# A graph and expert kernel on one core: 96-column products in its sort, table products in two halves, statistics on ScalarE, and byte source rows

## The chip, the cores and the metric

The kernel runs on one core of a Trainium2 chip. A core has five engines with a queue of instructions each, and an engine takes its queue in order: TensorE (PE for matmuls, PEld for its weight loads), VectorE (DVE), ScalarE (ACT), GpSimd (POOL) and SyncE (SP, which only issues DMAs). Semaphores tie the queues together. The metric is the device time of one execution in microseconds (us); lower is better.

## What is computed

A node table `x` (6250 x 256) and 206,250 directed edges (100,000 pairs in both directions and one loop per node) go through two graph attention layers and a mixture of eight experts:

```python
def _gat_layer(x, src, dst, W, b, a, g, beta, N, concat):
    h = x @ W.T + b
    score = (h @ a[:d])[src] + (h @ a[d:])[dst]
    e = jnp.exp(-jax.nn.leaky_relu(score, ALPHA))
    h_prime = jax.ops.segment_sum(e[:, None] * h[dst], src, num_segments=N)
    ...                      # a layer norm of each row, times g, plus beta
x = x + elu(gat(elu(concat(8 heads of gat(layernorm(x))))))
x = x + moe(layernorm(x))    # 8 experts, the best 2 of a softmax for each row
```

The edges are given sorted by `dst`; the sums go by `src`. So the kernel first sorts the edges by blocks of 128 sources.

## The kernel before

It has three stages in a row.

**The sort** (first 427 us) handles all edges in 23 segments (`SEGS`). For each segment DVE finds the edges of each of the 49 blocks (`rows_of_blocks`, L227, `here`), PE counts those in the rows before (`counts_before`, L234) and ACT copies the counts (L237, `up`). DVE weighs `here` with them (`places_before`, L244, `mine`), PE adds them up (`places`, L251), and DVE makes of the sum each edge's place in its run: `both_sides` reduces (L257), adds (L260), writes a one-hot `slot` of 84 places for each of 72 edge columns (L262), two products `what` (L266), and the addresses (L268, L271). Both tiles have their four columns of a group (`KC`) innermost, so a matmul reads them with a step of four f16 elements. `append` multiplies `what` by `slot` in 72 matmuls of 84 columns (L278), ACT copies the runs out of PSUM (L281), and POOL scatters them to `srt` in device memory by four indirect DMAs (L283), each of which waits for the one before to land.

In the same time the sort also makes the first layer's table: a `tick` moves each of the 49 blocks of `x` by one stage. ACT normalizes a block (`normed_x`, L344), PE transposes it (L349), ACT copies (L354), PE multiplies by the weights (`products`, L362: 512 columns of features to `ph` and 16 columns of scores to `pk`, f32, each as two passes for each of two halves of the depth, and a bias product, L363), and ACT copies the two results to `row` (L369, L370) and the scores to `s1` (L371); SP writes `row` to `tab1` (L372). Once for a chunk of seven blocks, `spread` takes mean and variance on DVE (L329, L330), adds epsilon (L332) and takes the root on ACT (L333); two ticks later `scales` makes reciprocal and shift (L337, L339).

The order is written out by hand. In iteration t the stages are emitted as places_before(t+2), rows_of_blocks(t+4), append(t), counts_before(t+3), places(t+2), both_sides(t+1), and after the second, the fourth and the sixth a tick, when one is due by this formula:

```python
if n % 2:
    due = len(ticks) * (3 * (t + 1) + n // 2) // (3 * SEGS)
```

`ticks` runs from -3 to 52; 56 ticks fall on 23 iterations, two or three on each. After the iterations 0, 5 and 10 stands a piece of `lefts` (L221, L222), some 9 us of small DVE operations.

**The two layers** (from 436 us to 2567 us and from 2613 us on) go through the sorted edges in tiles of 128, 34 tiles to a block, in groups of up to five (`GT`). `read_back` (L521) reads three blocks' worth of `srt`, splits source and destination numbers and writes the sources to `srow` (L546, L551). For a group, `sources` broadcasts its row of `srow` to all partitions (`rb`, L643, by SP), `gather` fetches each edge's table row by an indirect DMA on POOL for each tile (L649), `one_hot` compares `rb` with the partition number on DVE (`ot`, L656), PE picks the sources' scores with it (L662), DVE and ACT make the weights (L668, L670, L584, L585), DVE makes messages and a one-hot of destinations in the sum (L684, L687; in the second layer L693), and PE adds them up by source (L705). Stages of later groups are emitted ahead: the gathers six or eight groups, `one_hot` five, `sources` eleven. When a block is complete its layer norm and the next projection follow (L808 to L848 in the first layer); in the second layer the experts run in between (L1019, L1021, L1027).

Of the kernel before, what the change touches and what calls it, by code (L numbers as in the profile page):

```python
# [24 lines left out]
BF16 = mybir.dt.bfloat16  # L25
F16 = mybir.dt.float16
I32 = mybir.dt.int32
AF = mybir.ActivationFunctionType
OP = mybir.AluOpType
AX = mybir.AxisListType  # L30

P = 128
# [4 lines left out]
PITCH = 36  # L37
CHUNK = 18
RUN = 84
KC = 4  # L40


# [6 lines left out]
def kernel(ctx: ExitStack, tc: tile.TileContext, x, src, dst, w_heads, b_heads, a_heads,  # L49
# [20 lines left out]
    REST = E - FULL * EC  # L70
    LO = 2 * W
    PG = 7
    assert P - 16 < FULL < EP and LO < REST and W * PG <= 512
    CAP = TILES * P
    PIT = PITCH * P
    SLOTS = NB * PIT
# [10 lines left out]
    dram = ctx.enter_context(tc.tile_pool(name="dram", bufs=1, space=bass.MemoryType.DRAM))  # L87

    srt = dram.tile([2 * SLOTS + E + RUN, 1], F16, name="srt")
    srow = dram.tile([NB * PIT], BF16, name="srow")  # L90
    tab1 = dram.tile([NB * P + 1, R1], F32, name="tab1")
    ssrc1 = dram.tile([NB * P, H], F32, name="ssrc1")
    ssrc2 = dram.tile([NB * P, 1], F32, name="ssrc2")
# [18 lines left out]
    nc.gpsimd.iota(iota_n, pattern=[[1, P]], base=0, channel_multiplier=0, allow_small_or_imprecise_dtypes=True)  # L112
    iota_p = const.tile([P, 1], F32, name="iota_p")
    nc.gpsimd.iota(iota_p, pattern=[[0, 1]], base=0, channel_multiplier=1, allow_small_or_imprecise_dtypes=True)
    iota_e = const.tile([P, NE], F32, name="iota_e")
    nc.gpsimd.iota(iota_e, pattern=[[1, NE]], base=0, channel_multiplier=0, allow_small_or_imprecise_dtypes=True)
    zero = const.tile([1, R1], F32, name="zero")
# [135 lines left out]
    def both_sides(g):  # L253

        place = sw.tile([EP, W], F16, name="place")
        sums = sw.tile([EP, W], F32, name="sums")
        nc.vector.tensor_reduce(sums.rearrange("p (j k) -> p j k", k=KC),  # L257
                                seg[g]["pos"][:EP, :W * PG].rearrange("p (j b k) -> p j k b", b=PG, k=KC),
                                axis=AX.X, op=OP.add)
        nc.vector.tensor_add(place, sums, left[:, g * W:(g + 1) * W])  # L260
        slot = seg[g]["slot"] = sw.tile([EP, CHUNK, RUN, KC], F16, name="slot")
        nc.vector.tensor_tensor(slot, over(place.rearrange("p (j k) -> p j k", k=KC), RUN), each(place_no, RUN),  # L262
                                op=OP.is_equal)
        for i in range(2):
            what = whats[g % 2][:, :CHUNK * B2, :].rearrange("p (j b) k -> p j b k", b=B2)
            nc.vector.tensor_mul(what[:, :, i * NB:(i + 1) * NB, :], seg[g]["here"], over(by_column(kept[:, i], g), NB))  # L266
        c0 = g * KC
        nc.vector.tensor_tensor_scan(end[:B2, 1 + c0:1 + c0 + KC], count[:B2, c0:c0 + KC], count[:B2, c0:c0 + KC],  # L268
                                     initial=end[:B2, c0:c0 + 1], op0=OP.add, op1=OP.max)
        to = seg[g]["to"] = sw.tile([P, KC], I32, name="to", bufs=4)  # L270
        nc.vector.tensor_copy(to[:B2], end[:B2, c0:c0 + KC])  # L271

    def append(g):

        run_ps = bank("run", "run_ps")
        for k in range(KC):
            for j in range(CHUNK):
                nc.tensor.matmul(run_ps[:, k * RUN:(k + 1) * RUN], whats[g % 2][:, j * B2:j * B2 + P, k], seg[g]["slot"][:, j, :, k],  # L278
                                 start=(j == 0), stop=(j == CHUNK - 1))
        run = sw.tile([P, KC, RUN], F16, name="run", bufs=3)  # L280
        nc.scalar.copy(run[:B2].rearrange("p k r -> p (k r)"), run_ps[:B2, :KC * RUN])  # L281
        for k in range(KC):
            nc.gpsimd.indirect_dma_start(  # L283
                out=srt, out_offset=bass.IndirectOffsetOnAxis(ap=seg[g]["to"][:B2, k:k + 1], axis=0),
                in_=run[:B2, k, :], in_offset=None)
        seg[g] = None
# [28 lines left out]
    def load_x(c):  # L315
# [6 lines left out]
        nc.sync.dma_start(xc[:, :full, :], x[c0 * P:(c0 + full) * P, :].rearrange("(b p) f -> p b f", p=P))  # L322
        chunks[c] = {"x": xc}

    def spread(c):
        st = sw.tile([P, CB, nc.vector.BN_STATS_DIM], F32, name="st")
        mv = chunks[c]["mv"] = sw.tile([P, CB, 2], F32, name="mv")
        for i in range(CB):
            nc.vector.bn_stats(st[:, i, :], chunks[c]["x"][:, i, :])  # L329
            nc.vector.bn_aggr(mv[:, i, :], st[:, i, :])  # L330
        rstd = chunks[c]["rstd"] = sw.tile([P, CB], F32, name="rstd")
        nc.vector.tensor_scalar_add(rstd, mv[:, :, 1], EPS)  # L332
        nc.scalar.activation(rstd, rstd, AF.Sqrt)  # L333

    def scales(c):
        rstd = chunks[c]["rstd"]
        nc.vector.reciprocal(rstd, rstd)  # L337
        shift = chunks[c]["shift"] = sw.tile([P, CB], F32, name="shift")
        nc.vector.scalar_tensor_tensor(shift, chunks[c]["mv"][:, :, 0], -1.0, rstd, op0=OP.mult, op1=OP.mult)  # L339

    def normed_x(b):
        c, i = chunks[b // CB], b % CB
# [14 lines left out]
    def products(b):  # L357
        ph = bank("ph", "ph")
        pk = bank("pk", "pk")
        for to, cols in ((ph, slice(0, HD)), (pk[:, :2 * H], slice(HD, C1))):  # L360
            for k in range(KF):
                nc.tensor.matmul(to, blocks[b][:, k, :], wt[:, k, cols], start=(k == 0), stop=False)  # L362
            nc.tensor.matmul(to, three, bias3[:, cols], start=False, stop=True)  # L363
        blocks[b] = ph, pk

    def table_rows(b):
        ph, pk = blocks.pop(b)
        row = sw.tile([P, C1], F32, name="row", bufs=2)
        nc.scalar.copy(row[:, HD:], pk[:, :2 * H])  # L369
        nc.scalar.copy(row[:, :HD], ph)  # L370
        nc.scalar.copy(s1[:, b, :], row[:, R1:])  # L371
        nc.sync.dma_start(tab1[b * P:(b + 1) * P, :], row[:, :R1])  # L372

    def tick(n):

        for stage, behind in ((table_rows, 4), (products, 3), (turned_copy, 2), (turned_x, 1), (normed_x, 0)):
            if 0 <= n - behind < NB:
                stage(n - behind)
        if (n + 3) % CB == 0 and n + 3 < NB:
            spread((n + 3) // CB)  # L380
        if (n + 1) % CB == 0 and n + 1 < NB:
            scales((n + 1) // CB)
            if (n + 1) // CB + 1 < NB // CB:
                load_x((n + 1) // CB + 1)
# [29 lines left out]
    with tc.manual_schedule():  # L414
# [106 lines left out]
    def read_back(pool, c):  # L521
# [65 lines left out]
    def edges(es, layer, table, sel, ssrc, k, width, block_done, more=None):  # L587
# [573 lines left out]
```

## Time and profile before

| | |
|---|---|
| median of 14 runs | 4847.91 us (4839.64 to 4856.49) |
| the profiled execution | 4843.64 us, its span 4841.9 us |
| mean granted TensorE clock | 0.902 |
| PE, DVE, ACT, POOL busy | 80%, 67%, 27%, 70% of the span |
| last append of the sort, PE | 396.5 to 402.4 us |
| last scatter of the sort, POOL | starts at 426.3 us |
| first and last gather, layer 1 | start at 435.6 and 2566.5 us |
| first and last gather, layer 2 | start at 2613.0 and 4720.0 us |

A line of a group gives line of the kernel, engine, operation, what it writes and reads, shapes and count; after the bar the busy time in us and the mean of one in ns; after the second bar the idle time of the engine just before, and what ended it. A line of a timeline gives start, length, engine, line and operation. Consecutive operations of an engine overlap somewhat, so that the time from start to start can be shorter than the duration of one.

### The profile page before, as it was taken

The page shows a single profiled execution, that of the slowest core. Times are in us where ns is not written, and L with a number is a line of the kernel's source. Part 1 is how long each engine was busy: PE and PEld are TensorE (multiplying, and loading weights), DVE is VectorE, ACT ScalarE, POOL GpSimd, SP SyncE. Part 2 cuts the span into 40 slices and gives each one's busy share as a digit, 9 for nine tenths or more (in the row PEclk, how much of TensorE's full clock was granted, in tenths as well). Part 3 has the DMA queues.
Part 4 walks back from the last instruction along what each step waited for, and adds up shares of the span by engine and source line. Part 5 has one row for each costly group of instructions (what it writes and reads, how often), then busy time and mean ns, then how long its engine had stood idle before and what let it go on. Part 6 is the DMA issues. An engine that isn't in the chain of part 4 may idle for free. (4 is left out here: it accounts for less than half of the span.)

```text
span 4841.9 us, 52631 instructions
## 1 busy us (share of the span) xinstructions
PE 3886.2 (80%) x16462; PEld 2398.0 (50%) x16462; DVE 3259.3 (67%) x8048; ACT 1307.4 (27%) x2440; POOL 3368.0 (70%) x3450
## 2 busy tenths in 40 slices
PE   5995888888888888888885568778877877887888
PEld 3773343343334333343333456555655655655666
DVE  9995778788878887788774445555555555555553
ACT  1221111111111111111111124344433433433442
POOL 2455777777777777777774777777777777777770
PEclk7997999999999999999997779989988989989998
DMA  2214888888888888888885555555555555555540
GB/s 61 72 62 117 239 238 239 236 234 243 241 232 231 246 239 237 230 242 241 235 236 154 135 134 131 139 139 139 132 138 139 131 139 139 132 138 139 136 121 12
DMA packets 378009, 825.33 MB, mean 170 GB/s; under 512 B 91760, under 2 KB 210780, under 8 KB 377719
## 3 DMA queue, kind: packets, MB, share of 16 engines
q0 software_dynamic: 216464, 665.03, 51.5%
q1 hardware_dynamic: 155868, 151.02, 11.1%
q10 hardware_dynamic: 5386, 5.83, 0.4%
q8 instruction: 131, 2.15, 0.2%
q14 instruction: 160, 1.30, 0.1%
HBM read 792.59 MB, written 28.99 MB: 170 GB/s over the span
## 5 line engine op out<-in xcount | busy, mean ns | idle before, releaser
L649 POOL DMA_INDIRECT gt<-tab,dst_idx x3324 | 3181.4, 957 | 1104.8 <-issue 902.2
L705 PE MATMUL acc<-msg,hot 128*128 128x512 f32 x3324 | 1588.3, 629 | 0.0
L670 DVE TENSOR_TENSOR ssum<-ssum,gt 128x40 f32<-128x40 f32 (+3 forms) x684 | 126.9, 186 | 1323.8 <-DMA gt<-tab,dst_idx 1252.3
L705 PEld LDWEIGHTS acc<-msg,hot 128*128 128x128 f32 x3324 | 637.8, 201 | 684.0 <-issue 683.5
L687 DVE TENSOR_TENSOR msg<-gt,ee 128x2560 f32<-128x2560 f32 (+1 forms) x342 | 935.2, 2735 | 0.1
L705 PE MATMUL acc<-gt,hot 128*128 128x256 f32 x3324 | 920.8, 429 | 0.0
L705 PEld LDWEIGHTS acc<-gt,hot 128*128 128x128 f32 x3324 | 680.9, 214 | 100.3 <-issue 0.5
L585 ACT ACTIVATE ee<-lr 128x40 f32<-128x40 f32 (+3 forms) x684 | 141.7, 207 | 1667.2 <-DVE lr L584 1624.4
L585 ACT ACT_TABLE_LOAD x252 | 323.3, 1283 | 834.1 <-DVE lr L584 779.7
L1027 PE MATMUL py<-w2s,h 128*128 128x256 f32 x1568 | 407.1, 408 | 110.5 <-ACT h L1021 67.2
L662 PEld LDWEIGHTS <-ot 128*128 128x128 bf16 x3324 | 187.3, 100 | 588.9 <-issue 309.9
L693 DVE TENSOR_SCALAR hot<-iota_n,sloc,ee 128x128 f32<-128x128 f32 x1662 | 464.8, 357 | 0.9 <-issue 0.5
L662 PE MATMUL ps<-sel,ot 128*128 128x24 bf16 (+1 forms) x3324 | 187.8, 171 | 309.1 <-DVE ssum L668 297.1
L1019 PE MATMUL ph<-tokt,w1s 128*128 128x512 f32 (+1 forms) x832 | 378.0, 584 | 42.9 <-ACT h L1021 41.0
L1027 PEld LDWEIGHTS py<-w2s,h 128*128 128x128 f32 x1568 | 312.1, 203 | 189.9 <-ACT h L1021 75.2
L283 POOL DMA_INDIRECT srt<-run,to x92 | 170.6, 1854 | 245.6 <-DMA srt<-run,to 149.2
L825 PE MATMUL pt<-ident,hc 128*128 128x128 f32 x196 | 52.2, 418 | 285.2 <-DVE hc L821 285.2
L684 DVE TENSOR_TENSOR hot<-iota_ps,sloc 128x640 f32<-128x640 f32 (+1 forms) x342 | 272.8, 798 | 0.0
L656 DVE TENSOR_SCALAR ot<-rb,iota_p 128x640 bf16<-128x640 bf16 (+1 forms) x684 | 264.2, 387 | 7.3 <-DMA rb<-srow 7.3
L1019 PEld LDWEIGHTS ph<-tokt,w1s 128*128 128x128 f32 x832 | 152.8, 195 | 169.2 <-issue 106.1
L1032 DVE SCALAR_TENSOR_TENSOR xq<-py,comb,xq 128x256 f32<-128x256 f32 x392 | 166.8, 474 | 49.9 <-PE py L1027 49.9
L825 PEld LDWEIGHTS pt<-ident,hc 128*128 128x128 f32 x196 | 33.4, 208 | 325.3 <-DVE hc L821 325.3
(248 smaller groups left out, 3391.7 us busy)
## 6 DMA issues: line engine op xcount, KB each, us to landing
rb<-srow SPq DMA_DIRECT2D x588, 160.0 KB
gt<-tab,dst_idx POOLq DMA_INDIRECT x3324
tab<-row SPq DMA_DIRECT2D x49, 260.0 KB
rb<-srow SPq DMA_DIRECT2D x96, 128.0 KB
tab<-row SPq DMA_DIRECT2D x49, 128.5 KB
xq<-in_x_dram SPq DMA_DIRECT2D x12, 512.0 KB
out_dram<-xq SPq DMA_DIRECT2D x12, 512.0 KB
xc<-in_x_dram SPq DMA_DIRECT2D x6, 896.0 KB
```

The costliest lines, as they stand in the source:

```text
L283: nc.gpsimd.indirect_dma_start(out=srt, out_offset=bass.IndirectOffsetOnAxis(ap=seg[g]["to"][:B2, k:k + 1], axis=0), in_=run[:B2, k, :], i ...
L585: nc.scalar.activation(ee, lr, AF.Exp, scale=-1.0)
L649: nc.gpsimd.indirect_dma_start(out=gt[:, j, :], out_offset=None, in_=table, in_offset=bass.IndirectOffsetOnAxis(ap=dst_idx[c][:, t0 + j:t0 ...
L656: nc.vector.tensor_scalar(ot[:, :cols], now[n]["rb"][:, :cols], iota_p, None, op0=OP.is_equal)
L662: nc.tensor.matmul(ps[:, j * 3 * k:(j + 1) * 3 * k], ot[:, j * P:(j + 1) * P], sel[:, groups[n][0]].rearrange("p t k -> p (t k)"), start=T ...
L684: nc.vector.tensor_tensor(hot, iota_ps[:, None, :P].to_broadcast([P, nt, P]), sl[:, :, None].to_broadcast([P, nt, P]), op=OP.is_equal)
L687: nc.vector.tensor_mul(msg.rearrange("p j (h d) -> p j h d", h=k), gt[:, :, :width].rearrange("p j (h d) -> p j h d", h=k), ee[:, :, :, No ...
L693: nc.vector.tensor_scalar(hot[:, j, :], iota_n, sl[:, j:j + 1], ee[:, j, :], op0=OP.is_equal, op1=OP.mult)
L705: nc.tensor.matmul(accs[b][:, :width], now[n]["hot"][:, j, :], now[n]["msg"][:, j, :width], start=(g == 0 and j == 0), stop=False)
L1019: nc.tensor.matmul(ph[:, :W], w1s[:, e, k, f * P:(f + 1) * P], tokt[:, k, :W], start=(k == 0), stop=(k == KF - 1))
L1027: nc.tensor.matmul(py[:, (i - lo) * F:(i - lo + 1) * F], h1[:, k, i * P:(i + 1) * P], w2s[:, e, k, :], start=(k == 0), stop=(k == KF - 1))
L1032: nc.vector.scalar_tensor_tensor(xq[:, i, :], py[:, (i - lo) * F:(i - lo + 1) * F], comb[:, i, e:e + 1], xq[:, i, :], op0=OP.mult, op1=OP.add)
```

## The change

Four edits are made together.

- `append`'s matmuls read 96 columns of `slot` in place of 84. `slot` becomes a pair of fixed tiles with 12 columns of zeros at the end; the extra 12 columns of a matmul are the first of the next row and are written to PSUM and not copied out.
- `products` splits the 528 columns into two halves of 264 rather than 512 and 16; the copies follow.
- Mean and variance come from ACT: a new function `means` sums each block by an ACTIVATE with an accumulator, `spread` sums the squares of the difference in the same way. DVE scales the mean, and scales the sum of squares and adds epsilon. `means` is emitted in the tick two ahead of `spread` (for the first chunk in the same tick), at the end of the tick.
- `srow`, `lb` and `rb` hold bytes, not bf16; the byte is the source's number plus one, and `one_hot` compares it with a partition number plus one.

```diff
+RUN_N = 96
...
-    srow = dram.tile([NB * PIT], BF16, name="srow")
+    srow = dram.tile([NB * PIT], U8, name="srow")
...
+    nc.gpsimd.iota(iota_p1, pattern=[[0, 1]], base=1, channel_multiplier=1, allow_small_or_imprecise_dtypes=True)
...
+    slots = [sp.tile([EP, CHUNK * RUN + RUN_N - RUN, KC], F16, name=f"slot{i}") for i in range(2)]
...
-        slot = seg[g]["slot"] = sw.tile([EP, CHUNK, RUN, KC], F16, name="slot")
+        slot = seg[g]["slot"] = slots[g % 2]
...
-                nc.tensor.matmul(run_ps[:, k * RUN:(k + 1) * RUN], whats[g % 2][:, j * B2:j * B2 + P, k], seg[g]["slot"][:, j, :, k],
+                nc.tensor.matmul(run_ps[:, k * RUN_N:(k + 1) * RUN_N], whats[g % 2][:, j * B2:j * B2 + P, k],
+                                 seg[g]["slot"][:, j * RUN:j * RUN + RUN_N, k],
                                  start=(j == 0), stop=(j == CHUNK - 1))
...
-        nc.scalar.copy(run[:B2].rearrange("p k r -> p (k r)"), run_ps[:B2, :KC * RUN])
+        nc.scalar.copy(run[:B2], run_ps[:B2, :KC * RUN_N].rearrange("p (k r) -> p k r", r=RUN_N)[:, :, :RUN])
...
+    def means(c):
+        x = chunks[c]["x"]
+        mean = chunks[c]["mean"] = sw.tile([P, CB], F32, name="mean")
+        junk = sp.tile([P, F], BF16, name="junk")
+        for i in range(CB):
+            nc.scalar.activation(junk, x[:, i, :], AF.Identity, accum_out=mean[:, i:i + 1])
+        nc.vector.tensor_scalar_mul(mean, mean, -1.0 / F)
+
     def spread(c):
-        st = sw.tile([P, CB, nc.vector.BN_STATS_DIM], F32, name="st")
-        mv = chunks[c]["mv"] = sw.tile([P, CB, 2], F32, name="mv")
...
+        rstd = chunks[c]["rstd"] = sw.tile([P, CB], F32, name="rstd")
         for i in range(CB):
-            nc.vector.bn_stats(st[:, i, :], chunks[c]["x"][:, i, :])
-            nc.vector.bn_aggr(mv[:, i, :], st[:, i, :])
-        rstd = chunks[c]["rstd"] = sw.tile([P, CB], F32, name="rstd")
-        nc.vector.tensor_scalar_add(rstd, mv[:, :, 1], EPS)
+            nc.scalar.activation(junk, x[:, i, :], AF.Square, bias=mean[:, i:i + 1], accum_out=rstd[:, i:i + 1])
+        nc.vector.tensor_scalar(rstd, rstd, 1.0 / F, EPS, op0=OP.mult, op1=OP.add)
         nc.scalar.activation(rstd, rstd, AF.Sqrt)
...
-        for to, cols in ((ph, slice(0, HD)), (pk[:, :2 * H], slice(HD, C1))):
+        for to, cols in ((ph[:, :C1 // 2], slice(0, C1 // 2)), (pk[:, :C1 // 2], slice(C1 // 2, C1))):
...
+        if n == -3 or ((n + 5) % CB == 0 and n + 5 < NB):
+            means((n + 5) // CB)
         if (n + 3) % CB == 0 and n + 3 < NB:
             spread((n + 3) // CB)
...
+        for slot in slots:
+            nc.gpsimd.memset(slot[:, CHUNK * RUN:, :], 0.0)
...
-        lb = pool.tile([P, P], BF16, name="lb", bufs=2)
-        nc.vector.tensor_copy(lb[:n], lf[:n])
+        lb = pool.tile([P, P], U8, name="lb", bufs=2)
+        nc.vector.tensor_copy(lb[:n], own[:n])
...
-            rb = tile_of(n, "rb", [P, GT * P], RB, BF16)
+            rb = tile_of(n, "rb", [P, GT * P], RB, U8)
...
-            nc.vector.tensor_scalar(ot[:, :cols], now[n]["rb"][:, :cols], iota_p, None, op0=OP.is_equal)
+            nc.vector.tensor_scalar(ot[:, :cols], now[n]["rb"][:, :cols], iota_p1, None, op0=OP.is_equal)
```

More of the change, by code (lines that the diff above doesn't have):

```diff
@@ L27 @@
 I32 = mybir.dt.int32
+U8 = mybir.dt.uint8
 AF = mybir.ActivationFunctionType
@@ L72 @@
     PG = 7
-    assert P - 16 < FULL < EP and LO < REST and W * PG <= 512
+    assert P - 16 < FULL < EP and LO < REST and W * PG <= 512 and KC * RUN_N <= 512
     CAP = TILES * P
@@ L114 @@
     nc.gpsimd.iota(iota_p, pattern=[[0, 1]], base=0, channel_multiplier=1, allow_small_or_imprecise_dtypes=True)
+    iota_p1 = const.tile([P, 1], F32, name="iota_p1")
+    nc.gpsimd.iota(iota_p1, pattern=[[0, 1]], base=1, channel_multiplier=1, allow_small_or_imprecise_dtypes=True)
     iota_e = const.tile([P, NE], F32, name="iota_e")
@@ L260, in both_sides @@
         nc.vector.tensor_add(place, sums, left[:, g * W:(g + 1) * W])
-        slot = seg[g]["slot"] = sw.tile([EP, CHUNK, RUN, KC], F16, name="slot")
-        nc.vector.tensor_tensor(slot, over(place.rearrange("p (j k) -> p j k", k=KC), RUN), each(place_no, RUN),
-                                op=OP.is_equal)
+        slot = seg[g]["slot"] = slots[g % 2]
+        nc.vector.tensor_tensor(slot[:, :CHUNK * RUN, :].rearrange("p (j r) k -> p j r k", r=RUN),
+                                over(place.rearrange("p (j k) -> p j k", k=KC), RUN), each(place_no, RUN), op=OP.is_equal)
         for i in range(2):
@@ L323, in load_x @@
         chunks[c] = {"x": xc}
+    def means(c):
[5 more added lines that the diff above has]
+        nc.vector.tensor_scalar_mul(mean, mean, -1.0 / F)
     def spread(c):
-        st = sw.tile([P, CB, nc.vector.BN_STATS_DIM], F32, name="st")
-        mv = chunks[c]["mv"] = sw.tile([P, CB, 2], F32, name="mv")
+        x, mean = chunks[c]["x"], chunks[c]["mean"]
+        junk = sp.tile([P, F], BF16, name="junk")
+        rstd = chunks[c]["rstd"] = sw.tile([P, CB], F32, name="rstd")
         for i in range(CB):
-            nc.vector.bn_stats(st[:, i, :], chunks[c]["x"][:, i, :])
-            nc.vector.bn_aggr(mv[:, i, :], st[:, i, :])
-        rstd = chunks[c]["rstd"] = sw.tile([P, CB], F32, name="rstd")
-        nc.vector.tensor_scalar_add(rstd, mv[:, :, 1], EPS)
+            nc.scalar.activation(junk, x[:, i, :], AF.Square, bias=mean[:, i:i + 1], accum_out=rstd[:, i:i + 1])
+        nc.vector.tensor_scalar(rstd, rstd, 1.0 / F, EPS, op0=OP.mult, op1=OP.add)
         nc.scalar.activation(rstd, rstd, AF.Sqrt)
@@ L338, in scales @@
         shift = chunks[c]["shift"] = sw.tile([P, CB], F32, name="shift")
-        nc.vector.scalar_tensor_tensor(shift, chunks[c]["mv"][:, :, 0], -1.0, rstd, op0=OP.mult, op1=OP.mult)
+        nc.vector.tensor_mul(shift, chunks[c]["mean"], rstd)
     def normed_x(b):
@@ L368, in table_rows @@
         row = sw.tile([P, C1], F32, name="row", bufs=2)
-        nc.scalar.copy(row[:, HD:], pk[:, :2 * H])
-        nc.scalar.copy(row[:, :HD], ph)
+        nc.scalar.copy(row[:, :C1 // 2], ph[:, :C1 // 2])
+        nc.scalar.copy(row[:, C1 // 2:], pk[:, :C1 // 2])
         nc.scalar.copy(s1[:, b, :], row[:, R1:])
```

## The prediction

> **What bounds the kernel now.** I read the windows table first, then the groups of the first 560 us, their waits, and the timeline of one stretch. The windows table (columns: busy time and instructions of PE, PEld, DVE, ACT, POOL, then granted clock, DMA share, GB/s) shows two regimes.
>
> ```profile
> 320.00:340.00 20.00, 20.00 (x148) 14.20 (x147) 19.66 (x24) 7.02 (x24) 10.62 (x5) 1.00 0.17 59
> 380.00:400.00 20.00, 20.00 (x166) 15.30 (x165) 9.67 (x16) 5.24 (x19) 8.60 (x6) 1.00 0.25 75
> 420.00:440.00 20.00, 0.59 (x2) 0.29 (x2) 3.75 (x17) 0.00 (x0) 6.34 (x7) 0.50 0.19 48
> 1640.00:1740.00 100.00, 85.55 (x283) 40.30 (x282) 83.52 (x135) 17.66 (x42) 74.34 (x79) 0.95 0.89 240
> 4040.00:4140.00 100.00, 78.74 (x367) 58.41 (x367) 56.77 (x232) 36.73 (x55) 75.94 (x80) 0.91 0.53 141
> ```
>
> From 436 us on, both layers run at the pace of POOL: 79 to 80 gathers in 100 us, 0.946 us each and 0.305 us between them, whatever PE and DVE do. So the layers begin when the sort ends, and what the sort gains or loses moves everything. In the sort (0 to 427 us) PE and DVE are both full, ACT is a quarter to a third busy.
>
> ```profile
> L283 POOL DMA_INDIRECT srt<-run,to x92 | 170.6, 1854 | 245.6 <-DMA srt<-run,to 149.2 <-ACT run L281 52.7 <-DVE st L329 11.8
> L278 PE MATMUL run_ps<-slot,what 127*128 127x84 f16 x1656 | 135.8, 260 | 16.5 <-DVE what L266 16.5
> L362 PE MATMUL ph<-wt,xt 128*128 128x512 f32 x196 | 93.3, 598 | 0.0
> L266 DVE TENSOR_TENSOR what<-here,kept 127x3528 f16<-127x3528 f16 x46 | 89.6, 1989 | 0.0
> L262 DVE TENSOR_TENSOR slot<-place,place_no 127x6048 f16<-127x6048 f16 x23 | 76.1, 3309 | 0.8
> L362 PE MATMUL pk<-wt,xt 128*128 128x16 f32 x196 | 25.2, 242 | 0.0
> L329 DVE BATCH_NORM_STATS2 st<-xc 128x6 f32<-128x256 f32 x49 | 19.5, 398 | 0.0
> ```
>
> DVE hardly waits for PE here (0.0 and 0.8 us before L266 and L262): it runs ahead of PE by 0 to 9 us. PE and ACT are tied together instead, as the waits of 100 to 410 us show (engine line waited for: total us, times, longest):
>
> ```profile
> ACT run L281 <- PE run_ps L278: 153.3, 20, 10.7
> POOL srt L283 <- DMA srt<-run,to: 129.4, 63, 5.5
> PE run_ps L278 <- DVE what L266: 4.3, 3, 1.9
> ```
>
> DVE's lead decides this change. One iteration (t = 8), at the statistics of chunk 3:
>
> ```profile
> 187.29 5.90 PE L278 MATMUL run_ps<-slot,what 127*128 127x84 f16 x72
> 187.56 1.99 DVE L227 TENSOR_TENSOR here<-dig,block_no 127x3528 f16<-127x3528 f16 x1
> 189.47 0.42 DVE L329 BATCH_NORM_STATS2 st<-xc 128x6 f32<-128x256 f32 x1
> ...
> 193.23 0.44 ACT L281 CAST run<-run_ps 98x336 f16<-98x336 f32 x1 [8.59 <-PE run_ps L278]
> 193.39 0.67 DVE L257 TENSOR_REDUCE sums<-pos 127x72 f32<-127x504 f32 x1
> ...
> 195.88 0.63 ACT L344 ACTIVATE xn<-xc,shift,rstd 128x256 f32<-128x256 f32 x1
> ...
> 197.17 1.68 PE L251 MATMUL pos<-mine,eye 127*128 127x504 f16 x7
> ```
>
> DVE takes the statistics at 189.5 us and goes on to both_sides at 193.4, while ACT comes to the end of the same tick only at 196.5, because its copies stand behind PE's append and counts.
>
> **Part 1, halves of 264.** From start to start a 512-column f32 pass takes 0.429 us, a 16-column one 0.111, the two bias products 0.220 and 0.025. Before, a block costs 4 x 0.429 + 0.220 + 0.363 + 0.025 = 2.33 us. After: L1027's 256 columns start 0.216 apart, so 264 take 0.223; 8 x 0.223 + 2 x 0.113 = 2.01. Saved 0.32 x 49 = **-15.7 us** of PE. ACT copies the same 528 columns (0.48 + 0.07 us before, about 0.6 after): nothing.
>
> **Part 2, statistics on ACT.** DVE sheds 49 pairs of L329 and L330, 0.53 us from pair to pair: 26 us. ACT gains 98 ACTIVATEs of 128x256. L923 (the same shape, no pointer) takes 0.417 us, L344 (two pointers) 0.623, neighbours overlap by 0.1; the accumulator's read is not in this trace. Seven means cost 2.3 to 3.9 us, I take 3.0; seven squares 3.7. ACT has room for these 47 us. But DVE's L332 (and a new scaling of the mean) now wait for ACT **in the same tick**, and behind them in DVE's queue stands the whole of both_sides, for which PE's next append waits. Where the tick lies between counts_before and places (as above), the cost counts from the end of PE's counts: 1.8 us until ACT ends its tick (194.7 to 196.5), 3.0 or 3.7 of statistics, 0.2 on DVE, 8.1 for both_sides (193.39 to 201.48): 13.1 or 13.8. In that time PE has only places (1.68) and two or three ticks of 2.27: 6.2 or 8.5. By the tick formula this falls on t = 2 (squares, two ticks: 7.6 us of waiting), 5 (squares, three: 5.3), 7 (means, two: 6.9), 8 (squares, three: 5.3), 10 (means, three: 4.6): 29.7. The other statistics come ahead of append or at the end of an iteration, with 15 us of PE work to hide them. At t = 5 and 10 the lefts follow (9.2 us of DVE), which DVE's lead had covered: from there 21.5 us on DVE against 16.1 on PE, 5.4 twice = 10.8. ACT's Sqrt after the lefts now comes late for the transposes, some 5. Sum 45.5, less the 5.7 that PE waited ahead of append before (at t = 2, 3, 7 and 12, over the usual 0.11): **+40 us**. A cheaper accumulator takes off 3, a dearer one adds 5.
>
> **Part 3, 96 columns.** 72 matmuls of L278 take 5.90 us, 80 ns each from start to start, at the full clock and at half of it alike (t = 0 ran at 0.5). So the array's clock doesn't set it. If the load of what does, 96 cost nothing; if the read of slot does, 80 x 96/84 = 91 ns, 0.8 us a segment, +16; if the longer stream runs as the 196 columns of L234 do (86 ns), 42 ns. I take 80, as the row itself has it; both ends stay. L281 copies the same 336 elements, and the padding's two memsets and the new iota run on POOL in the first 20 us, ahead of its first scatter at 63.8: nothing. The Trainium skill (TensorE: Matmul & The Clock Gate, Back-to-back issue gap) gives 81 ns for a load and 128 columns in a stream, by which 96 would be free and the sum stays; by the row's proportion it would be 16 more. As a general floor the trace contradicts it: 24 columns of L662 start 25 ns apart.
>
> **Part 4, bytes.** L656 takes 379 ns for 640 two-byte elements. The mixed-width rows L531 and L546 (128 elements in 285 and 220 ns) run at two elements a cycle, which makes L656 about 545; at one a cycle (as L183, 1656 in 1884 ns) it would be 880. I take 545. That is 0.17 us in a group of 6.3 us where DVE idles 17% in layer 1, more in layer 2: hidden. The Trainium skill (VectorE: DVE Perf Modes, What auto-detection actually checks) asks for two-byte operands on both sides for four elements a cycle, so by it the op falls to two, as I take it; no row here has a byte operand, and if width made no difference the layers would come to -4. Not hidden is POOL: 35 gathers of layer 1 and 66 of layer 2 are stretched until an L656 that runs across their start has ended (12.6 us in all; the scatters are stretched by the f16 TENSOR_TENSORs in the same way, up to 4.62 us). With L656 0.17 us longer each hit grows by so much and some are added: +7 and +13. At one element a cycle it may no longer hold POOL up (no row tells), then the 12.6 go: bounds -13 and +30. Half the bytes: a 1280-byte packet takes 55 ns of a queue, 1024 take 46, 256 take 18; so 640 about 32, 3% of layer 1's DMA share. Layer 1 loses 45 us in 49 waits for landings, one each block, at DMA 0.88; I credit -4 (0 to -15).
>
> **The sum.** PE reaches the last append 40 - 15.7 = 24 us later. The scatters end at 427.3, 24.9 us after PE, and idle DVE time lets them catch up a little: -3 (bounds -10 and 0). Sort +21, layers +16: the profiled run of 4843.64 (span 4841.9 and 1.7 around it) becomes 4881; the median of the runs shown lies 4.3 above it, so **4885 us**.
>
> **Rivals.**
> 1. *The 96-column stream is fast* (42 ns). Append falls from 5.9 to 3.1 us, 2.8 in each of some 15 chains that hold an append: -42, PE ends 18 earlier than before. DVE's own cycle of 12.2 us and the scatters (about 3 in such a cycle) then hold it to about -8; with the bytes +16: 4856, not slower by what can be measured, and 4823 if L656 also stops holding POOL up. It decides from about 45 ns down. For it: 80 ns is far over what the columns need. Against: strided operands, and no row with such a count. Chance 0.24.
> 2. *Bytes at one element a cycle, POOL not held up*, columns not fast: 4848 + 21 - 17 = 4852. Chance 0.1.
> 3. *The change doesn't do what it says on ACT*: the waits are absorbed since the scatters, not PE, end last. POOL's chain is full from t = 3; if it drains as fast as DVE idles, sort +0, total 4864. Against: 25 us exceed its backlog of 16. Chance 0.1.
> 4. *91 ns and a dear accumulator*: 4885 + 16 + 5 = 4906. The forecast's mechanism at its dear end; chance 0.2.
> The forecast itself 0.36, with a range of its own of 4868 to 4900.
>
> **The numbers.** What a measurement can tell from no change is 0.2%, 9.7 us. Faster needs rival 1 and an L656 that holds POOL less: 0.15. Within: the rest of rivals 1 and 2: 0.19. Slower: the forecast, rivals 3 and 4: 0.66. The range takes in rival 1's middle and rival 4: 4834 to 4912.
>
> **What the new profile should show.** L278's spacing (80, 91 or 42 ns); DVE's waits for ACT at the scaling and at rstd, and PE's for what, at t = 3, 6, 8, 9, 11 and 12; the first gather near 457 us instead of 435.6; L656 near 545 ns; POOL's long gathers more numerous in layer 2. Wrong would be: DVE not waiting for ACT, an accumulator under 0.3 us, or L278 far from 80.

## The result and the profile after

The changed kernel takes **4909.35 us** (median of 6 runs, 4903.72 to 4918.42) against 4847.34 us of the kernel before (median of 28): ratio 1.013, 95% interval 1.012 to 1.0141. Its profiled span is 4906.2 us, 64.3 more than before, at a granted clock of 0.896. To read the numbers below, one fact of the chips is needed. Ten of the twelve experiment runs fell on three chips on which the kernel before itself takes 5627 to 5676 us at a clock of 0.84 and POOL is not what paces the layers; the last two fell on a chip where it takes 4903 us. Each ratio is against the kernel before on the same chip. Between chips I compare only the sort (PE's last append starts at 441.7, 442.2 and 441.4 us in three runs of the same sort, on three chips) and lengths of operations.

The windows of the kernel after, with the columns of those of before:

```profile
320.00:340.00 20.00, 20.00 (x165) 17.09 (x163) 17.51 (x17) 12.14 (x39) 11.51 (x6) 1.00 0.16 55
380.00:400.00 20.00, 20.00 (x156) 16.70 (x154) 19.83 (x17) 8.90 (x28) 9.84 (x5) 1.00 0.17 56
460.00:480.00 20.00, 4.12 (x16) 2.35 (x14) 6.98 (x30) 0.00 (x0) 7.32 (x8) 0.50 0.28 75
1640.00:1740.00 100.00, 85.12 (x283) 40.65 (x282) 84.32 (x136) 16.31 (x41) 75.24 (x79) 0.95 0.84 224
4040.00:4140.00 100.00, 78.42 (x363) 58.91 (x364) 55.90 (x210) 43.65 (x61) 76.24 (x79) 0.90 0.51 127
```

The layers still run at POOL's pace, 79 gathers in 100 us. But the empty stretch that stood at 420 to 440 us now stands at 460 to 480: the sort ends later. The first gather starts at 473.1 us (435.6 before, +37.5). Layer 1 lasts 2144.5 us from first to last gather (+13.6), the stretch between the layers 41.6 (-4.9), layer 2 2125.1 (+18.1), and what follows is the same 121.9. The sum is +64.3.

The groups of the first 560 us of the kernel after:

```profile
L283 PE MATMUL run_ps<-slot,what 127*128 127x96 f16 x1656 | 152.9, 270 | 15.2 <-DVE what L271 15.2
L289 POOL DMA_INDIRECT srt<-run,to x92 | 145.2, 1578 | 308.3 <-ACT run L287 135.9 <-DMA srt<-run,to 127.1 <-ACT up L242 19.3
L376 PE MATMUL ph<-wt,xt 128*128 128x264 f32 x196 | 57.4, 419 | 0.0
L256 PE MATMUL pos<-mine,eye 127*128 127x504 f16 x161 | 51.4, 472 | 47.1 <-DVE sums L262 35.8 <-DVE mine L249 11.2
L376 PE MATMUL pk<-wt,xt 128*128 128x264 f32 x196 | 52.3, 389 | 0.0
L345 ACT ACTIVATE junk<-xc,mean 128x256 bf16<-128x256 f32 x49 | 24.8, 507 | 6.4 <-DVE mean L337 5.0
L336 ACT ACTIVATE junk<-xc 128x256 bf16<-128x256 f32 x49 | 20.4, 415 | 1.3
```

L278 has become L283, and its 1656 matmuls are busy 17 us longer (135.8 before). POOL's scatters (L289), which waited mostly for one another before, now wait most for ACT's copy and so for PE (135.9 us, 52.7 before). The waits of 100 to 410 us name the cause (engine line waited for: total us, times, longest):

```profile
DVE rstd L346 <- ACT junk L345: 39.4, 5, 11.8
DVE mean L337 <- ACT junk L336: 34.5, 5, 11.4
PE pos L256 <- DVE sums L262: 27.6, 6, 4.9
```

DVE, which hardly waited before, stands still ten times for ACT's statistics, and PE six times for DVE. One such place is the tick of t = 8 that the prediction drew (timeline):

```profile
225.49 0.75 PEld L376 LDWEIGHTS pk<-wt,xt 128*128 128x128 f32 x4
...
226.56 0.50 ACT L345 ACTIVATE junk<-xc,mean 128x256 bf16<-128x256 f32 x1
...
230.76 0.19 ACT L345 ACTIVATION_READ_ACCUMULATOR junk<-xc,mean 128x1 f32 x1
230.98 0.17 DVE L346 TENSOR_SCALAR rstd<-rstd 128x7 f32<-128x7 f32 x1 [10.36 <-ACT junk L345]
231.06 0.67 DVE L262 TENSOR_REDUCE sums<-pos 127x72 f32<-127x504 f32 x1
...
231.79 3.10 PE L256 MATMUL pos<-mine,eye 127*128 127x504 f16 x7 [4.79 <-DVE sums L262]
```

DVE has stood idle for 10.36 us when L346 starts: L346 stands ahead of L262 in its queue and waits for the end of ACT's tick and then for seven squares, 4.4 us. PE then waits 4.79 us at `places`, not at `append`: the kernel has one `pos` bank, and the reduce must have read it. And the seven matmuls of `pos` take 3.10 us, where they took 1.68 before. The windows around this wait show why (same columns):

```profile
223.00:227.00 4.00, 3.99 (x33) 3.37 (x31) 0.00 (x0) 2.64 (x9) 1.61 (x2) 1.00 0.04 8
...
231.80:235.80 4.00, 4.00 (x12) 2.02 (x12) 3.96 (x3) 1.11 (x4) 1.01 (x1) 0.59 0.19 71
235.80:239.00 3.20, 3.20 (x19) 2.53 (x18) 3.20 (x2) 1.73 (x5) 0.00 (x0) 1.00 0.21 81
```

The granted clock is 1.00 ahead of the wait, 0.59 in the four microseconds behind it and 1.00 after that. The same follows each of the seven waits of 4.1 to 4.9 us, with 0.50 in the other six. The Trainium skill (TensorE: Matmul & The Clock Gate, What's actually happening) says that an idle window of about 3.4 us halves the clock until about as long a busy one has passed; behind these seven waits this trace agrees, and I had not applied it. But a wait need not be that long. In the kernel before, PE waited 1.93 and 1.68 us ahead of the appends at 110.89 and 251.40 us, and the windows behind them show half the clock too:

```profile
112.40:115.80 3.40, 3.40 (x46) 3.40 (x44) 3.37 (x5) 0.00 (x0) 3.40 (x1) 0.50 0.00 0
252.40:255.70 3.30, 3.30 (x45) 3.30 (x43) 3.27 (x4) 0.00 (x0) 3.21 (x1) 0.50 0.00 0
```

### The profile page after: what moved, and what is told of

It is laid out like the page before. It is cut to its first block, busy times and chain, and to the rows that moved or that the text cites. A ratio compares the mean times of both kernels' runs of the same rounds, so it can differ in the third digit from the quotient of the medians.

```text
span 4906.2 us, 52733 instructions
## 1 busy us (share of the span) xinstructions
PE 3916.9 (80%) x16462; PEld 2442.8 (50%) x16462; DVE 3341.9 (68%) x7957; ACT 1365.4 (28%) x2636; POOL 3379.8 (69%) x3453
## 5 line engine op out<-in xcount | busy, mean ns | idle before, releaser
L667 POOL DMA_INDIRECT gt<-tab,dst_idx x3324 | 3218.4, 968 | 1094.7 <-issue 938.0
L705 DVE TENSOR_TENSOR msg<-gt,ee 128x2560 f32<-128x2560 f32 (+1 forms) x342 | 935.1, 2734 | 0.0
L1037 PE MATMUL ph<-tokt,w1s 128*128 128x512 f32 (+1 forms) x832 | 379.7, 586 | 39.1 <-ACT h L1039 35.9
L674 DVE TENSOR_SCALAR ot<-rb,iota_p 128x640 bf16<-128x640 uint8 (+1 forms) x684 | 372.4, 545 | 10.8 <-DMA rb<-srow 10.8
L289 POOL DMA_INDIRECT srt<-run,to x92 | 145.2, 1578 | 308.3 <-ACT run L287 135.9
```

The costliest lines, as they stand in the source:

```text
L289: nc.gpsimd.indirect_dma_start(out=srt, out_offset=bass.IndirectOffsetOnAxis(ap=seg[g]["to"][:B2, k:k + 1], axis=0), in_=run[:B2, k, :], i ...
L667: nc.gpsimd.indirect_dma_start(out=gt[:, j, :], out_offset=None, in_=table, in_offset=bass.IndirectOffsetOnAxis(ap=dst_idx[c][:, t0 + j:t0 ...
L705: nc.vector.tensor_mul(msg.rearrange("p j (h d) -> p j h d", h=k), gt[:, :, :width].rearrange("p j (h d) -> p j h d", h=k), ee[:, :, :, No ...
L1037: nc.tensor.matmul(ph[:, :W], w1s[:, e, k, f * P:(f + 1) * P], tokt[:, k, :W], start=(k == 0), stop=(k == KF - 1))
```

## Experiments on the statistics

The theory: it is the place of DVE's small instructions in its queue that costs PE some 45 us. The rival: it is ACT's own extra work, or the other parts.

**Statistics back on DVE**, the other three parts kept:

```diff
-            nc.scalar.activation(junk, x[:, i, :], AF.Square, bias=mean[:, i:i + 1], accum_out=rstd[:, i:i + 1])
+            nc.vector.bn_stats(st[:, i, :], chunks[c]["x"][:, i, :])
+            nc.vector.bn_aggr(mv[:, i, :], st[:, i, :])
```

> The kernel after, with x's statistics back on DVE (bn_stats and bn_aggr), the other parts kept. Theory: the waits of DVE for ACT inside a tick cost PE about 45 us, and they go: the jumps between append starts at t = 3, 6, 7, 8, 9, 11 and 12 disappear, PE waits for what at most 6 us, last append 441.7 -> 394 to 400, first gather 473.1 -> 432 to 438 (the scatters end some 27 us behind PE), layers unchanged, time 4909 -> 4868 to 4876. Rival, that the delay of the sort is the 96 columns' and the copies' on ACT: the last append stays above 420, time 4890 or more.

PE's last append starts at 397.2 us, the first gather at 435.5; ratio 0.9963 (0.9945 to 0.998). So the statistics cost PE 441.7 - 397.2 = **44.5 us**, and all 37 of the sort's end. (The ratio is under 1 because on these chips the bytes shorten the layers, see below.)

**Statistics on ACT alone**, the other parts kept. The factor of the mean and the variance's factor and epsilon go into ACT's own instructions, so no DVE instruction waits in the tick:

```diff
-            nc.scalar.activation(junk, x[:, i, :], AF.Identity, accum_out=mean[:, i:i + 1])
-        nc.vector.tensor_scalar_mul(mean, mean, -1.0 / F)
+            nc.scalar.activation(junk, x[:, i, :], AF.Identity, scale=-1.0 / F, accum_out=mean[:, i:i + 1])
...
-        nc.vector.tensor_scalar(rstd, rstd, 1.0 / F, EPS, op0=OP.mult, op1=OP.add)
-        nc.scalar.activation(rstd, rstd, AF.Sqrt)
+        nc.scalar.activation(rstd, rstd, AF.Sqrt, scale=1.0 / F, bias=eps)
```

> The kernel after, with the same 98 ACTIVATEs with accumulator on ACT, but the two small DVE instructions behind them taken out: the mean's factor goes into the ACTIVATE's scale, the variance's factor and EPS into the Sqrt's scale and bias, so DVE no longer waits for ACT in the middle of a tick (it still takes the reciprocal two ticks later). Theory (place, not work): ACT is as busy as in the kernel after, but the jumps between append starts go, last append 441.7 -> 395 to 405, first gather 473 -> 432 to 442, time 4909 -> 4868 to 4880. Rival (ACT's own 45 us of work hold up its copies, and PE by them): last append 425 or later, time 4893 or more. Layers unchanged.

Last append 395.0, first gather 436.6, ratio 0.9957 (0.9938 to 0.9976): the rival falls. The windows from 100 to 380 us of the kernels before, after, and with ACT alone, in this order, show the same:

```profile
100.00:380.00 280.00, 274.32 (x2288) 211.84 (x2286) 261.84 (x336) 80.17 (x265) 136.94 (x69) 0.99 0.21 67
```

```profile
100.00:380.00 280.00, 245.15 (x1930) 206.46 (x1928) 203.36 (x230) 111.40 (x371) 91.63 (x60) 0.92 0.18 59
```

```profile
100.00:380.00 280.00, 271.75 (x2267) 235.72 (x2266) 238.04 (x248) 126.70 (x420) 136.12 (x68) 0.99 0.21 67
```

With ACT alone ACT is busier than in the kernel after (126.7 to 111.4 us), yet PE idles 8 us instead of 35 and its clock is back at 0.99. DVE still waits for ACT, 25.1 us in nine waits for the copy of the counts (6.0 before), but at places where it costs PE nothing. Of the 44.5 us, 29.2 are thus PE's added idle time (274.32 - 245.15). The rest shows in the length of the same matmuls in the first 560 us; these are the groups with ACT alone, to be held against those of the kernel after above:

```profile
L376 PE MATMUL ph<-wt,xt 128*128 128x264 f32 x196 | 52.5, 391 | 0.0
L258 PE MATMUL pos<-mine,eye 127*128 127x504 f16 x161 | 41.4, 398 | 18.1 <-DVE mine L251 11.2 <-DVE sums L264 6.9
```

In the kernel after, `pos` is busy 10.0 us longer and `ph` 4.9 us, with small changes in the others some 16 us: the halved clock, which went with the waits.

## Experiments on the 96 columns

**84 columns again**, the other parts kept (`RUN_N = 84`, no padding):

> The kernel after, with 84 columns for 96 in the rows' products. Theory: the read of slot sets a matmul's time, so the spacing falls from 90 ns to 80 and the 23 appends of 72 matmuls lose 72 x 10 ns x 23 = 16.6 us of PE; some of it is swallowed where PE waits for DVE anyway. Last append 441.7 us -> 427 to 431, first gather 473.1 -> 460 to 464, time 4909 -> 4895 to 4900. Rival, that PE's waits for DVE swallow nearly all: spacing 80 but the last append at 437 or later, time 4904 or more. Rival, that the spacing has another cause: it stays at 90 ns, time 4909. The layers keep their spans (2144.5 and 2125.1 us).

Spacing 80 ns, last append 430.6 (-11.1), first gather 469.4 (3.7 to 7.5 earlier than 473.1, 475.0 and 476.9 of the same sort with 96), ratio 1.0027 (1.0007 to 1.0047). PE got what was expected; the end got less than the 9 expected at the least, since the last scatter now starts 23.6 us behind the end of PE's last append, not 15.4 as in the kernel after. Without the waits the same edit is worth more on PE: 395.0 with 96 columns and ACT alone, 379.9 with 84 (further below), 15.1 us.

**What sets the time of a matmul.** Eight rows of 36 extra matmuls ahead of one append of the kernel before; the first, the second and the sixth:

```diff
+            for i in range(36):
+                nc.tensor.matmul(run_ps[:, :96], wf[:, 16 * i:16 * i + 512:4], sf[:, 16 * i:16 * i + 384:4], start=True, stop=True)
+                nc.tensor.matmul(run_ps[:, :96], wf[:, 16 * i:16 * i + 512:4], sf[:, 16 * i:16 * i + 96], start=True, stop=True)
+                nc.tensor.matmul(run_ps[:, :48], wf[:, 16 * i:16 * i + 512:4], sf[:, 16 * i:16 * i + 192:4], start=True, stop=True)
```

> The kernel before with eight rows of 36 extra matmuls each ahead of the append of segment 15, into the same PSUM tile and overwritten by it (their products are used by nobody): it measures a matmul's time from start to start by the width and the step of its two operands. Step 4 is 8 bytes, as in the append. Theory (the read of slot with a step of 8 bytes sets the time): 96 columns with step 4 90 ns, 128 with step 4 120, 48 with step 4 45 to 55 (then the weight load may set it); 96 dense columns 42 to 60 ns, the same with a dense and with a stepped weight. Rival (the stepped weight load sets it): a dense weight with stepped columns falls below 70 ns, and the stepped weight with dense columns stays at 80 to 90. Rival (the number of columns alone): 96 dense columns 90 ns as well. Time about 25 us over the kernel before, less what PE waits for anyway.

The timeline of PE, one line for each row of 36:

```profile
296.85 3.42 PE L280 MATMUL run_ps<-slot,what 127*128 127x96 f16 x36
300.09 1.71 PE L282 MATMUL run_ps<-slot,what 127*128 127x96 f16 x36
301.64 3.31 PE L284 MATMUL run_ps<-slot,what 127*128 127x96 f16 x36
304.77 1.71 PE L286 MATMUL run_ps<-slot,what 127*128 127x96 f16 x36
306.32 4.42 PE L288 MATMUL run_ps<-slot,what 127*128 127x128 f16 x36
310.56 1.91 PE L290 MATMUL run_ps<-slot,what 127*128 127x48 f16 x36
312.28 1.84 PE L292 MATMUL run_ps<-slot,what 127*128 127x96 f16 x36
313.96 2.17 PE L294 MATMUL run_ps<-slot,what 127*128 127x128 f16 x36
```

From start to start, by columns, step of the columns and step of the weight (in elements of two bytes):

| columns | step | weight step | ns |
|---|---|---|---|
| 96 | 4 | 4 | 90 |
| 96 | 1 | 4 | 42 |
| 96 | 4 | 1 | 87 |
| 96 | 1 | 1 | 42 |
| 128 | 4 | 4 | 118 |
| 48 | 4 | 4 | 48 |
| 96 | 2 | 4 | 46 |
| 128 | 1 | 1 | 56 |

It is the read of `slot` with its step of 8 bytes, 0.92 to 0.94 ns a column from 96 on, twice the dense price; a step of 4 bytes costs almost nothing, and the weight's step hardly matters (90 to 87 ns). Both rivals fall. The Trainium skill (TensorE: Matmul & The Clock Gate, Back-to-back issue gap) gives, for a matmul by itself, the width over 2.4 plus 2.5 ns at the full clock: the dense rows, each matmul with its own weight load, agree (42 and 56), and the stepped rows show what it leaves out.

## Experiments on the bytes

**BF16 rows again**, the other parts kept (`srow`, `lb`, `rb` in BF16, compared with `iota_p`):

> The kernel after, with the rows of sources in BF16 as before, the other parts kept. Theory: L674 falls from 546 to 379 ns, POOL's long gathers fall back (about 35 to 60 in layer 1 and 66 to 213 in layer 2 by the limit used), the layers take 2131 and 2107 us for 2144.5 and 2125.1, the sort stays: first gather 473, time 4909 -> 4880 to 4884. Rival, that the layers are longer for another cause than the bytes (the later start, the clock): they keep 2144 and 2125, time 4909. Rival, that the smaller transfers hid a gain: layer 1's waits for landings rise from 38 to 44 us; this alone would be 6 us the other way, and is in the theory's sum.

The excess of the gathers is the sum of what each takes over 0.946 us. L674 takes 380 ns, and the excess is 20.5 us in layer 1 and 33.0 in layer 2, against 28 to 31 and 67 to 76 in the three kernels with bytes of the same call. The ratio is 1.0076 (1.0055 to 1.0097), some 43 us, hardly more than its sort's 38 to 41. On these chips the layers' time does not follow the excess: in layer 1 POOL waits some 440 to 500 us beyond its usual 0.305 us a gather anyway, mostly for DVE's messages (L705) to free a buffer.

**Bytes alone in the kernel before, and F32 rows alone**, to tell the length of L656 from the width of its source:

```diff
-            rb = tile_of(n, "rb", [P, GT * P], RB, BF16)
+            rb = tile_of(n, "rb", [P, GT * P], RB, U8)
```

> The kernel before with the rows of sources as bytes alone (80 KB for 160 in a load, L656's source one byte wide). Theory (POOL's gathers wait for the longer L656): the sort keeps its 435.6 us to the first gather; in layer 1 the gathers' excess over 0.946 us rises from 9.6 to about 29 us and the waits for landings fall by about 6, in layer 2 the excess rises from 27.3 to about 45; layers together +26 to +32 us, ratio 1.0050 to 1.0068 where the kernel before takes 4847 us. Rival, that the layers' 27 us of the kernel after came from the later start or the lower clock: layers within 6 us of before, ratio under 1.0015. Rival, that half the bytes pay: ratio under 0.999.

> The kernel before with the rows of sources as F32 (320 KB for 160 in a load): L656's source is four bytes wide, so by the rows with mixed widths it also runs at two elements a cycle, 546 ns instead of 379, but the DMA moves more instead of less. It tells length from width. Theory (the length of L656 counts, not the byte): layer 2, where DMA has room, shows the same +17 to +19 us in the gathers' excess as the kernel after (27.3 -> 45); layer 1 shows that too, and 10 to 25 us more in waits for landings, since its DMA share of 0.88 goes up. Rival (a byte source is what holds POOL up): layer 2's excess stays within 5 us of 27.3. Time by the theory 4890 to 4910 (ratio 1.009 to 1.013), by the rival 4855 to 4875.

> Once more the kernel before with the rows of sources as bytes alone, for a chip on which the kernel before takes about 4847 us. Theory (POOL's gathers wait for the longer L656, and POOL paces the layers): excess of the gathers over 0.946 us 27 to 31 us in layer 1 and 43 to 48 in layer 2 (9.6 and 27.3 before), layer 1 +10 to +16 us, layer 2 +15 to +20, first gather within 3 us of 435.6, ratio 1.0050 to 1.0070. Rival (the 27 us came with the later start or the clock): layers within 6 us, ratio under 1.0015. Where the kernel before takes 5600 us or more, POOL is not what paces the layers (waits of 440 to 490 us before its gathers in layer 1), the excess rises all the same, and the time falls by 0.2 to 0.6% as in the first look.

The groups of the kernel with bytes, then of the one with F32 rows:

```profile
L652 POOL DMA_INDIRECT gt<-tab,dst_idx x3324 | 3245.3, 976 | 1788.8 <-issue 986.9
...
L659 DVE TENSOR_SCALAR ot<-rb,iota_p 128x640 bf16<-128x640 uint8 (+1 forms) x684 | 370.5, 542 | 11.6 <-DMA rb<-srow 11.6
```

```profile
L649 POOL DMA_INDIRECT gt<-tab,dst_idx x3324 | 3246.4, 977 | 1776.5 <-issue 1000.1
...
L656 DVE TENSOR_SCALAR ot<-rb,iota_p 128x640 bf16<-128x640 f32 (+1 forms) x684 | 372.1, 544 | 11.4 <-DMA rb<-srow 11.2
```

Byte or four bytes, the operation takes the same time, and POOL's gathers lengthen alike: excess 31.2 and 33.6 us in layer 1, 69.6 and 68.3 in layer 2, where BF16 rows on the same chip show 18.8 and 32.2. So the length of L656 holds POOL up, not the width. One such gather in the kernel after:

```profile
953.82 0.54 DVE L674 TENSOR_SCALAR ot<-rb,iota_p 128x640 bf16<-128x640 uint8 x1
953.95 1.23 POOL L667 DMA_INDIRECT gt<-tab,dst_idx  x1 [0.30 <-issue]
```

The gather ends 0.82 us after the end of the comparison that runs across its start. In the kernel before 89 of the gathers over 0.97 us end 0.80 to 0.83 us after an L656, with 12.4 us of excess; in the kernel after it is 189, with 39.9 us.

The times on these chips went the other way than expected: 0.9957 (0.994 to 0.9974) and 0.9952 (0.9935 to 0.9969) with bytes, 0.9961 (0.9943 to 0.9978) with F32. That F32 rows, four times as large as rows of bytes, gain as much shows that the gain does not come from moving less; its cause stays open.

**The kernel after once more**, on the chip where before takes 4903 us:

> The kernel after, unchanged, on a chip of the kind on which the kernel before takes some 5650 us and the single edits were timed; it gives them their common reference. Theory (the sort is the same there, and its edits add up): first gather 470 to 477 us against 436 to 442 of a kernel with the sort of before, +34 to +38; the bytes' layers -0.43 to -0.48% as measured alone (-25 us): together +9 to +13, ratio 1.0015 to 1.0035. Rival (the layers lose with the bytes there too): +60 or more, ratio 1.010 or more.

The ratio is 1.0126 (1.0108 to 1.0144), 62.2 us: what the rival said, since this chip is not of the kind that my numbers assumed. First gather 475.0, so some 39 us are the sort's and 23 the layers', if the kernel before has its first gather at 435.6 here too. The last experiment below ran in the same call with BF16 rows: it shows an excess of 9.6 and 29.4 us where the kernel after has 27.8 and 41.2. Layer 2, where both have 80 gathers in 100 us, lasts 2109.1 us with BF16 rows and 2122.7 with bytes: where POOL paces the layer, bytes cost 13.6 us.

Layer 1 went the other way, 2198.1 us with BF16 rows and 2189.3 with bytes: there POOL waits 140.1 us for landings of earlier gathers with BF16 rows and 111.2 with bytes. From the first gather to the end the two profiled executions take 4477.9 and 4475.5 us, so they don't show the 20 us that the medians of the two kernels leave for the layers (79.9 apart, 59.8 of it ahead of the first gather). What bytes cost the whole kernel on this chip is thus not settled.

## A version that is faster

**Before with halves and ACT alone** (84 columns, BF16 rows), run twice:

```diff
-        for to, cols in ((ph, slice(0, HD)), (pk[:, :2 * H], slice(HD, C1))):
+        for to, cols in ((ph[:, :C1 // 2], slice(0, C1 // 2)), (pk[:, :C1 // 2], slice(C1 // 2, C1))):
...
+        nc.scalar.activation(rstd, rstd, AF.Sqrt, scale=1.0 / F, bias=eps)
```

> The kernel before (84 columns, BF16 rows) with the tables' columns in two halves and x's statistics on ACT without any DVE instruction behind them until the reciprocal. Theory: PE saves 0.32 us in each of 49 blocks and DVE 26 us, no new wait stands in DVE's queue; last append 396.5 -> 378 to 386. The scatters then end the sort: they need about 3.9 us each (92 of them from 63.8 us on), so the first gather comes no earlier than 422 (435.6 before): time -6 to -13 us, ratio 0.9973 to 0.9988. Rival, that ACT's 45 us delay PE as in the kernel after: last append over 400, ratio 1.0005 or more. Layers unchanged.

> Once more the kernel before with halves and x's statistics wholly on ACT (84 columns, BF16 rows), for a chip on which the kernel before takes about 4847 us. In the first look its last append started at 379.9 us and its first gather at 421.6 (396.5 and 435.6 before). Theory (the sort's end moves the whole program, the layers are the same): -11 to -16 us, ratio 0.9967 to 0.9978. Rival (the layers give it back, as they depend on when they start): ratio 0.999 or more.

Last append 379.9 and 379.7 (397 to 398 in the sort of before on these chips), first gather 421.6 and 429.4 (436.7 to 442.2); ratio 0.9987 (0.997 to 1.0004) and 0.9992 (0.9975 to 1.0009). The sort gains as expected; the whole can't be told from no change there, and the runs don't settle what takes the gain back.

**The same with `slot` in pairs**, so that the columns are read with a step of 4 bytes:

```diff
-        slot = seg[g]["slot"] = sw.tile([EP, CHUNK, RUN, KC], F16, name="slot")
+        slot = seg[g]["slot"] = sw.tile([EP, 2, CHUNK, RUN, 2], F16, name="slot")
...
-                nc.tensor.matmul(run_ps[:, k * RUN:(k + 1) * RUN], whats[g % 2][:, j * B2:j * B2 + P, k], seg[g]["slot"][:, j, :, k],
+                nc.tensor.matmul(run_ps[:, k * RUN:(k + 1) * RUN], whats[g % 2][:, j * B2:j * B2 + P, k], seg[g]["slot"][:, k // 2, j, :, k % 2],
```

> The kernel with halves and x's statistics wholly on ACT, and slot laid out in pairs of k, so that the append's columns are read with a step of 4 bytes instead of 8 (DVE writes it in two instructions of 3024 elements instead of one of 6048). By the probe a matmul then takes 46 to 48 ns instead of 80: an append 3.3 to 3.5 us instead of 5.9, 56 us of PE in all. Theory (PE no longer ends the sort; DVE's cycle of some 12 us and the 92 scatters at 3.9 us do): spacing 46 to 48 ns, last append 360 to 376 (379.9 before), first gather 418 to 430 (421.6 and 429.4 before), ratio within 0.0015 of that kernel's 0.9987 and 0.9992. Rival (PE ends the sort): last append 340 or earlier, first gather under 405, ratio under 0.996. If DVE's pairs run at one element a cycle, slot takes 6.3 us instead of 3.3 and the last append comes at 410 or later.

The groups and waits of its sort:

```profile
L288 POOL DMA_INDIRECT srt<-run,to x92 | 155.2, 1687 | 240.5 <-DMA srt<-run,to 140.1 <-ACT run L286 64.8 <-ACT up L239 9.7
...
L266 DVE TENSOR_TENSOR slot<-place,place_no 127x3024 f16<-127x3024 f16 x46 | 77.8, 1733 | 0.8
L283 PE MATMUL run_ps<-slot,what 127*128 127x84 f16 x1656 | 76.5, 211 | 15.4 <-DVE what L271 15.3
```

```profile
ACT run L286 <- DMA srt<-run,to: 42.5, 5, 11.6
```

Spacing 41 ns, a little under the 46 expected; DVE pays nothing for writing `slot` in two (77.8 us to 76.1). PE's busy time in append falls from 135.8 to 76.5 us, but the last append only moves from 380 to 368.5 and the first gather to 415.2: ACT now waits for run buffers that scatters hold, so DVE and the scatters end the sort, as the theory had it. The first gather and the ratio came out better than the theory's range, though: the ratio is **0.9957** (0.9943 to 0.9971), faster than both kernels. That is 21 us less than 4903, and the first gather is 20.4 us earlier than 435.6.

## Why the prediction was right in direction and 24 us short

I said 4885, it is 4909.35: inside the range of 4834 to 4912, near its end, and outside the 4868 to 4900 that I gave the forecast itself. The sort was +37.5 for my +21, the layers +26.7 for my +16. That makes 27 us; 3 go off again because I set the median 4.3 us above the profiled run, and after the change it lies 1.4 above.

- **Halves, -15.7 us.** Right: at the full clock a block takes 2.01 to 2.04 us from start to start (2.33 before), which makes 14 to 16. Halves alone weren't run.
- **Statistics, +40 us.** The mechanism held at the places named, and the size came out at 44.5. But that it came so near is luck: two errors cancelled inside it. I had 45.5 us of waits: PE waits mainly for the reduce (L262), ahead of `pos`, not for the whole of both_sides, ahead of the append (there it waits 1.64 us at most from the third append on), and lefts and the late Sqrt cost 4.9 and 4.28 us instead of 15.8, so the seven long waits came to 31.8. And I had no term for the clock, which adds some 13 to 16. The accumulators were at my dear end: seven means take 3.8 us, seven squares 4.4, as each ACTIVATE has an accumulator read of 187 ns behind it.
- **96 columns, 0.** This is the mis-sized step: "I take 80, as the row itself has it". It is 90 ns, 72 x 23 x 10 ns = 16.6 us of PE, which I had priced in rival 4 and set aside. The row at half clock had rightly said that the array doesn't set the 80 ns; it could not tell the weight load from the read of `slot`. Nor could the 86 ns for 196 columns of L234, whose columns have a step of 1, but whose weight has no step either; it showed only that a step was what differed. With 80 ns the sum puts the read's 16 us at nothing; the rows with one step each, which tell the two apart, came with the probe. Rival 1's 42 ns is the dense price and never applied.
- **Sum on PE.** 44.5 + 16.6 - 15.7 = 45.4; the last append is 45.2 us later. The scatter tail then took back 8.5 us (23.9 before, 15.4 after, from the end of PE's last append to the start of the last scatter), within the bounds of my -3. Rival 3, that it takes back everything, fell.
- **Bytes.** L656's 545 ns came out (546). POOL's stretch was sized too small: I had +7 and +13, the gathers' excess grew by 19.5 us in layer 1 (9.6 to 29.1; gathers over 0.97 us from 59 to 186) and 17.5 in layer 2 (27.3 to 44.8; 213 to 261). I had lengthened mainly the hits that were there, but an operation 1.4 times as long also hits more often: the gathers that end 0.80 to 0.83 us after an L656 grow from 28 to 69 in layer 1 and from 61 to 120 in layer 2, and make 27.5 of the 37.0 us. Layer 1's waits fell by 6 us and the stretch between the layers by 5, more than my -4; that the fewer bytes did this was not tested. Nor did the kernel after run with BF16 rows on a chip of the first kind, so that the layers' +26.7 are all the bytes' rests on these counts and on layer 2 of the run above.
- **Rival 4** names its two causes, 91 ns and a dear accumulator; its 4906 is nearest to the result, though the bytes' part of the gap was in no rival.

## What to carry over

An operation moved to an idle engine is cheap only if nothing in the full engine's queue waits for its result at once: here two small DVE instructions for each chunk of seven blocks cost PE 44.5 us, and folded into ACT's own scale and bias they cost it nothing. Price a matmul by the step of its moving columns as well as by their number, and look for the step before adding columns or taking them away. Where a wait of 4 us on PE is added, add the slow clock behind it, here some 2 us for each.

## What the runs showed of the hardware

- f16 columns read by a matmul with a step of 8 bytes cost 0.92 to 0.94 ns each (90 ns for 96, 118 for 128), with a step of 4 bytes 0.48, dense 0.44; the step of the weight changes 90 to 87 ns at most.
- In the 4 us after a PE wait of 4.1 to 4.9 us the granted clock is 0.50 to 0.59: seven `pos` matmuls then take 3.10 us instead of 1.68. It also fell to 0.50 for 3.4 us behind waits of 1.93 and 1.68 us.
- A DVE comparison of 640 elements takes 379 ns from BF16 and 542 to 546 from bytes or F32, and POOL's indirect DMAs are held up by its length, not by the width: a gather that it holds up ends some 0.82 us after it; alone a gather takes 0.946 us.
- An ACTIVATE with accumulator over 128x256 takes 415 ns (507 with a bias and Square) and its accumulator read 187 more, 0.54 and 0.63 us from one to the next.
